# Layer norms' last step on VectorE or ScalarE, and a new order for a two-layer graph network

## The chip, the cores and the metric

The kernel runs on one core of a Trainium2 chip. The metric is the device time of one execution in microseconds (us), and the median of several executions is quoted. The core's engines work side by side, each through its own list of instructions in order: TensorE (PE in the profile, its weight loads PEld), VectorE (DVE), ScalarE (ACT), GpSimd (POOL) and SyncE (SP), which only issues DMAs here.

## The reference

Two graph layers run one after the other over 16 graphs of 1024 nodes with 256 features. The second layer has two attention steps and a feed-forward network.

```python
# layer 0, w = 16, n = 1024, d = 256, H = 8 heads of 32
q, k, v = heads(features @ Wq), heads(features @ Wk), heads(features @ Wv)
e = einsum(q, k); e = where(e >= 0, e, 0.2 * e)
attn = softmax(where(adj > 0, e, NEG)); h = attn @ v
out = layernorm(h, g1, b1)
out = concatenate([out, features]) @ Wffn.T
x = layernorm(out, g2, b2) + features
# layer 1, gat: Wh = h @ W, scores = leaky(Wh @ a[:d] + (Wh @ a[d:]).T), softmax over axis 1
h = gat(gat(x, adj, W1, a1), adj, W2, a2)
h = layernorm(x + h, g_ln1, b_ln1)
ff = relu(h @ w_ff1 + b_ff1) @ w_ff2 + b_ff2
out = layernorm(h + ff, g_ln2, b_ln2)
# layernorm: (x - mean) * rsqrt(var + eps) * g + b, over the 256 features
```

There are four layer norms. The first three are followed in the kernel by a transpose, after which gain and offset are applied by column; the last one goes to the output.

## The kernel before, in words

A graph is called a batch `b`. Its 1024 nodes are 8 tiles of 128 rows, or 4 pairs `u` of tiles.

**The work of a batch.** `x_pair` loads and transposes the features, `mask_part` packs the adjacency matrix into an fp8 mask, and `qk_part` and `v_part` make queries, keys and values. Queries and keys go through DRAM and come back as split halves (`load_stacks`). For each of 8 heads and 8 key tiles, `all_scores` makes a 128x1024 score tile on PE (L615). `weights` scales it on ACT (L631), takes the maximum on DVE (L633), takes the exponential on ACT (L636) and multiplies by the mask on POOL (L640). `all_values` multiplies the weights by the values and by minus one (L655), which is done in 32-column pieces ("narrow" in the planner). `join` adds two weight tiles on DVE (L699). `after_head` brings a head's result into `hn`.

Then comes the rest of the batch (`rest`). `rows_pair` normalizes `hn` (first layer norm), transposes it (L372), multiplies by `Wffn` (L792, L795), normalizes the result `y` (second layer norm), transposes it and forms `x1` and the rows of the first attention (L824). `attention` makes a 128x1024 weight tile per node tile on DVE (L877, L880) and scales the rows on ACT (L885). `second_rows` (L915) and `normed_pair` (L940) are the products of the two attentions. `normed_pair` ends with the third layer norm and a transpose into `rT`. `feed_forward` and `hidden` (L980, L986, L989, L1008) work on `rT`, and end in the fourth layer norm, which has lines of its own (L1019, L1021).

**Layer norms.** `stats` makes mean and variance by row on DVE (L350, L352) and the reciprocal deviation `rs` on ACT by a logarithm and an exponential (L355, L357). `normalized` (L361 to L366) then does one DVE instruction per 128x256 tile: subtract the mean, multiply by `rs`. It is called for two tiles at a time, three times per pair `u`: on `hn` and on `y` in `rows_pair`, and on `y` in `normed_pair`. That is 3 x 4 x 16 = 192 calls and 384 tiles.

**What sets the order.** Each engine's list is written before the program runs, by a planner (`Order`). Every piece of work is a thread, a Python generator, that asks for an engine with a planned duration in ns (`on(DVE=320, shared=True)`), for a buffer of a pool (`take`, `give`), or for another thread's event (`wait`, `fire`). Where a thread offers two engines, the planner takes the one that would end first by its own clocks, and the instruction is emitted for that engine. `shared` says that DVE and POOL exclude each other in the plan for that instruction. Among all pieces that could start within 300 ns of the earliest, the one with the smallest due time (`aim`) goes first. The due times are a batch's start plus a table entry times `SLOT` (253 us in the table before): `AIM` for steady batches, `EARLY` for the rest of batches 0 and 1. In the tables, `rows`, `first0/1`, `graph0/1`, `second`, `normed` and `ff` are the stages of `rest`; `x`, `mask`, `qk`, `v` are the next batch's preparation; `fast0`, `fast1` and `fast15` stretch the due times of the scores in those batches; `lead` is how far ahead of its due time a score may go. `ff` has one entry per pair `u`, the wait after the third layer norm before its feed-forward is due. A changed duration or table entry can thus change the order of all five lists.

**Pools.** PSUM has 2 score buffers, 1 accumulator for the values and 3 general ones (`misc`). SBUF has 6 buffers for weights (`p`), 18 small ones (`pair`), and 1 `job`, held by the feed-forward that runs.

Of the kernel before, what the change touches and what calls it, by code (L numbers as in the profile page):

```python
# [14 lines left out]
AF = mybir.ActivationFunctionType  # L15
OP = mybir.AluOpType
# [170 lines left out]
def on(shared=False, delay=0.0, mode=None, **costs):  # L187
    return "on", (costs, shared, delay, mode)
# [22 lines left out]
def start(thread, aim):  # L211
    return "start", (thread, aim)


def aim(time, lead):
    return "aim", (time, lead)
# [17 lines left out]
def unshifted_path(  # L234
# [8 lines left out]
    nc = tc.nc  # L243
# [16 lines left out]
    YW = D + 2  # L260
    NSUM = NT * H + 2 * NT
    NSCORE = 4 * NT
    SLOT = 253e3
    PACE = SLOT / (H * NT // 2)


    AIM = dict(mask0=0.602, x=1.454, x_step=-0.0104, mask=0.9396, mask_step=-0.0101, qk0=0.4907, qk1=1.7441,
               qk_step=-0.0518, v0=0.7416, v1=0.621, v_step=0.0547, rows=-0.079, rows_step=-0.0113, first0=0.2137,
               first1=-0.446, graph0=-0.0793, graph1=0.316, graph_step=0.0481, second=0.7493, second_step=-0.015,
               normed=1.0223, normed_step=-0.0115, ff_wait=(None, 0, 1, 0), ff=(0.5532, 0.1074, 3.6996, 1.0353),  # L270
               ff_step=0.0063, fast0=0.2312, fast1=0.6979, fast15=1.0127, lead=14.8372)

    EARLY = dict(x=2.6481, x_step=-0.1001, mask=0.5019, mask_step=0.0795, qk0=0.7532, qk1=1.2626, qk_step=-0.1325,
                 v0=0.2134, v1=1.5023, v_step=-0.0416, rows=-2.7213, rows_step=-0.3343, first0=-0.8482,
                 first1=-4.695, graph0=0.0441, graph1=-0.9035, graph_step=-0.1073, second=0.463,
                 second_step=0.0554, normed=0.7744, normed_step=0.0342, ff_wait=(None, 0, 1, 0),
                 ff=(2.0875, 0.7055, 1.5112, 0.6358), ff_step=0.0607)

    const = ctx.enter_context(tc.tile_pool(name="const", bufs=1))
    sb = ctx.enter_context(tc.tile_pool(name="sb", bufs=1))  # L280
# [7 lines left out]
    def share(b, name):  # L288
        return (EARLY if b < 2 else AIM)[name]

# [67 lines left out]
        return mv, rs  # L358

    def normalized(dst, srcs, mv, rs):  # L360
        for i, (row, src) in enumerate(zip(dst, srcs)):  # L361
            if row is src:
                yield on(DVE=320, shared=True)
            else:
                yield on(DVE=323)
            nc.vector.tensor_scalar(row, src, mv[:, i, 0:1], rs[:, i:i + 1], op0=OP.subtract, op1=OP.mult)  # L366

    def transposes(pt, srcs):

# [34 lines left out]
    def mask_part(b, t, halves):  # L404

        n = len(halves)
        ints = []
        if b:
            yield take("adj")
        elif halves[0]:  # L410
            yield wait(("mask", b, t, 0))
        for kh in halves:
            yield take("pair")
            ai = buf([P, HALF], "pair", "adj_i", I32)
            ints.append(ai)
            part = adj[b].rearrange("(u p i) k -> u i p k", p=P, i=2)[t // 2, t % 2, :, kh * HALF:(kh + 1) * HALF]
            if b:
                yield pause(1500)
                yield on(ACT=400, delay=3500)
                nc.scalar.dma_start(ai, part)  # L420
            else:
                yield pause(2000)
                yield load()
                nc.sync.dma_start(ai, part)
        yield take("adjb")
        ab = buf([P, 2 * HALF], "adjb", "adj_b", F8)
        for i, ai in enumerate(ints):
            yield on(DVE=336, shared=True)
            nc.vector.tensor_scalar(ab[:, i * HALF:(i + 1) * HALF], ai, 0.0, -1.0,
                                    op0=OP.is_gt, op1=OP.mult, saturate=False)  # L430
            yield give("pair")
        if b:
            yield give("adj")
        yield take("misc")
        pt = misc(BF)
        pairs = ab.bitcast(BF)
        yield on(PE=30 + 140 * n)
        for i in range(2 * n):
            nc.tensor.transpose(pt[:, i * P:(i + 1) * P], pairs[:, i * P:(i + 1) * P], ident_b)
        yield give("adjb")  # L440
        yield on(ACT=46 + 218 * n)
        k0 = 2 * halves[0]
        nc.scalar.copy(masks[b].bitcast(BF).rearrange("p (k q) -> p k q", k=NP)[:, k0:k0 + 2 * n, t * P:(t + 1) * P],
                       pt[:, :2 * n * P].rearrange("p (k q) -> p k q", k=2 * n))
        yield give("misc")
        for kh in halves:
            yield fire(("mask", b, t, kh))

    def make_mask(b, t0):
# [3 lines left out]
        for n, (t, halves) in enumerate(parts):  # L453
            yield start(mask_part(b, t, halves),
                        t0 + ((share(b - 1, "mask") if b else AIM["mask0"]) + share(b - 1, "mask_step") * n) * SLOT)

# [4 lines left out]
    def x_pair(b, u):  # L461
        yield take("pair")
        xr = buf([P, 2, D], "pair", "xr")
        yield pause(1500)
        yield on(ACT=400, delay=3500)
        nc.scalar.dma_start(xr, x[b, u * 2 * P:(u + 1) * 2 * P, :].rearrange("(p i) d -> p i d", p=P))
        yield take("misc")
        pt = misc()
        yield on(PE=460)
        transposes(pt, [xr[:, i, :] for i in range(2)])  # L470
        yield give("pair")
        engine = yield evacuate(2 * D)
        copy(engine, xTs[b][:, :, u * 2 * P:(u + 1) * 2 * P], pt.rearrange("p (c n) -> p c n", c=DC))
        yield give("misc")
        yield fire(("xT", b, u))

    def qk_part(b, g, o, nh):

        w = (wq, wk)[o]
        cols = slice(nh * HALF, (nh + 1) * HALF)  # L480
        for u in range(nh * 2, nh * 2 + 2):
            yield wait(("xT", b, u))
        if b:
            yield take("stage")
        yield take("pair")
        yield take("pair")
        yield take("misc")
        pa = misc()
        high, low = (buf([P, HALF], "pair", n) for n in ("high", "low"))
        yield on(PE=1728)  # L490
        for dc in range(DC):
            nc.tensor.matmul(pa, w[:, dc, g * P:(g + 1) * P], xTs[b][:, dc, cols],  # L492
                             start=(dc == 0), stop=(dc == DC - 1))
        yield on(ACT=466)
        nc.scalar.copy(high.bitcast(FR), pa)
        yield on(DVE=594)
        nc.vector.tensor_tensor(low, pa, high, op=OP.subtract)
        yield give("misc")
        if (b, g) == (0, 1):

            yield wait(("stack", 0, 0))
        yield load(2)
        for i, part in enumerate((high, low)):
            nc.sync.dma_start(scratch[b, g][o, :, i, cols], part)
        yield give("pair")
        yield give("pair")
        if b:
            yield give("stage")
        yield fire(("qk", b, g, o, nh))

    def project_qk(b, g, t0):
        scratch[b, g] = dram.tile([2, P, 2, N], FT, name="qk_halves")
        for o in range(2):
            for nh in range(NH):
                yield start(qk_part(b, g, o, nh), t0 + (2 * o + nh) * share(b - 1, "qk_step") * SLOT)

    def v_part(b, g, u):
        yield wait(("xT", b, u))
        yield take("misc")
        pa = misc()  # L520
        yield on(PE=895)
        for i in range(2):
            for dc in range(DC):
                nc.tensor.matmul(pa[:, i * P:(i + 1) * P], xTs[b][:, dc, (2 * u + i) * P:(2 * u + i + 1) * P],  # L524
                                 wv[:, dc, g * P:(g + 1) * P], start=(dc == 0), stop=(dc == DC - 1))
        engine = yield evacuate(2 * P)

        dst = vs[b, g][:, 2 * u:2 * u + 2, :].rearrange("p t c -> p (t c)")
        src = pa[:, :2 * P]
        if engine == "DVE":  # L530
            nc.vector.tensor_scalar(dst, src, -1.0, None, op0=OP.mult)
        else:
            nc.scalar.activation(dst, src, AF.Copy, scale=-1.0)
        yield give("misc")
        yield fire(("v", b, g, u))

    def project_v(b, g, t0):
        yield take("v")
        vs[b, g] = buf([P, NT, G * DH], "v", "v")
        for u in range(NP):  # L540
            yield start(v_part(b, g, u), t0 + share(b - 1, "v_step") * u * SLOT)

# [6 lines left out]
    def project(b, t0):  # L549
        yield take("xT")  # L550
        xTs[b] = buf([P, DC, N], "xT", "xT")
        for u in range(NP):
            yield start(x_pair(b, u), t0 + (share(b - 1, "x") + share(b - 1, "x_step") * u if b else 0.0) * SLOT)
        yield start(make_mask(b, t0), t0 + (0.5 if b else 0.0) * SLOT)
        for g in range(H // G):
# [35 lines left out]
    def pace(b):  # L591
        return PACE * {0: AIM["fast0"], 1: AIM["fast1"], B - 1: AIM["fast15"]}.get(b, 1.0)

    def all_scores():
        for b in range(B):
# [4 lines left out]
            for h in range(H):  # L600
                yield wait(("stack", b, h))
                q, kk = stacks[b, h]
                for t in range(NT):
                    due = t0 + (h * NT + t) / 2 * pace(b)
                    if b == 0 or t % 2 == 0:
                        yield aim(due, AIM["lead"] * PACE)
                        for _ in range(2 if b else 1):
# [877 lines left out]
```

## Time and profile before

| what | value |
|---|---|
| median of 3 runs | 4314.74 us (4314.66 to 4316.35) |
| the profiled execution's own time | 4317.81 us |
| its span, first to last instruction | 4315.9 us |
| mean granted TensorE clock | 0.990 |
| instructions | 76274 |
| first score of batch 0, 1, 2 | 39.1, 208.0, 468.8 us |
| first score to first score, batches 5 to 15 | 260.1 to 260.4 us each |
| last score | 4089.2 us |

The span is shorter than the execution by 1.9 us. The profile's first part gives each engine's busy time and its share of the span; the second part cuts the span into 40 equal slices and gives the busy share in tenths. Answers by stage give busy time of each engine in a stretch of the span. The waits are idle time of an engine, put down to the instruction that ended it. The groups give, by line, engine and tile, the count, the summed busy time and the mean duration in ns of one instruction.

### The profile page before, as it was taken

To read this page: it belongs to the slowest core of one execution; us is meant where nothing else is said; L and a number is where in the kernel's file an instruction comes from. 1 tells how busy PE (TensorE), PEld (TensorE's weight loads), DVE (VectorE), ACT (ScalarE), POOL (GpSimd) and SP (SyncE) were. 2 spreads that over 40 slices of the span, in tenths; PEclk is the share of its full clock that TensorE was granted. 3 is DMA by queue.
4 is the path that set the end of the run, shared out by engine and by line. 5 is a ranking of instruction groups with operands and counts; after the bars stand their busy time and mean duration, and the time that the engine had idled before them with its cause. 6 is when DMAs were issued, how large, how long until landed. Compare 5 with 4: busy or idle time off the path is not lost.

```text
span 4315.9 us, 76274 instructions
## 1 busy us (share of the span) xinstructions
PE 4189.7 (97%) x30027; PEld 3030.3 (70%) x30027; DVE 3544.8 (82%) x5491; ACT 2942.7 (68%) x4362; POOL 2571.6 (60%) x1161
## 2 busy tenths in 40 slices
PE   8788999999999999999999999999999999999999
PEld 4466677677777777777777777777777777777687
DVE  6878878888888887879879788887889879788853
ACT  6756677777767677776776767677776776767632
POOL 5846467664757656574664757646575674747700
PEclk9999999999999999999999999999999999999999
DMA  6413223322232322323232222322323222222100
GB/s 188 125 54 99 69 76 87 91 72 86 74 94 67 96 84 68 90 71 89 84 84 81 79 81 79 91 73 81 91 74 89 81 84 84 74 79 57 30 20 21
DMA packets 156282, 344.79 MB, mean 80 GB/s; under 512 B 21750, under 2 KB 24332, under 8 KB 155916
## 3 DMA queue, kind: packets, MB, share of 16 engines
q1 hardware_dynamic: 112140, 260.13, 21.0%
q10 hardware_dynamic: 43776, 79.71, 6.6%
q8 instruction: 239, 3.92, 0.4%
q14 instruction: 127, 1.04, 0.1%
HBM read 239.09 MB, written 100.66 MB: 79 GB/s over the span
## 4 chain that ended last, share of the span: by engine, by line
PE 82%; DVE 11%; ACT 3%; POOL 1%; DMA 1%; issue 1%; SPq 0%; ACTq 0%; POOLq 0%; DVEq 0%
PE ps_a L655 17%; PE ps_s L615 11%; PE ps_m L915 10%; PE ps_m L980 9%; PE ps_m L940 9%; PE ps_m L1008 7%; PE ps_m L492 4%; DVE p L633 3%; PE ps_m L792 3%; PE ps_m L824 3%; PE ps_m L795 3%; PE ps_m L524 2%; PE ps_m L372 2%; DVE p L699 2%; POOL p L640 1%; DVE att L880 1%
## 5 line engine op out<-in xcount | busy, mean ns | idle before, releaser
L640 POOL TENSOR_TENSOR p<-p,mask 128x1024 f32<-128x1024 f32 x1024 | 2471.1, 2431 | 1425.5 <-ACT p L636 1044.1
L633 DVE TENSOR_TENSOR p<-p,ps_s 128x1024 f32<-128x1024 f32 x1024 | 1211.3, 1213 | 251.2 <-ACT p L631 248.1
L636 ACT ACTIVATE p<-p 128x1024 f32<-128x1024 f32 x1024 | 1082.2, 1059 | 302.3 <-DVE p L633 276.7
L631 ACT ACTIVATE p<-ps_s 128x1024 f32<-128x1024 f32 x1006 | 986.3, 1021 | 345.2 <-PE ps_s L615 283.0
L615 PE MATMUL ps_s<-qs,ks 128*128 128x512 f32 x2048 | 658.7, 437 | 30.6 <-DVE p L633 27.0
L655 PE MATMUL ps_a<-p,v 128*32 128x256 f32 x8192 | 561.9, 388 | 24.4 <-POOL p L640 24.3
L615 PEld LDWEIGHTS ps_s<-qs,ks 128*128 128x128 f32 x2048 | 352.6, 190 | 266.1 <-issue 114.8
L940 PE MATMUL ps_m<-y,att 128*128 128x256 f32 x2048 | 481.1, 382 | 12.6 <-ACT y L885 11.1
L915 PE MATMUL ps_m<-y,att 128*128 128x258 f32 x2048 | 477.1, 383 | 14.4 <-ACT y L885 12.9
L980 PE MATMUL ps_m<-rT,wf 128*128 128x256 f32 x2048 | 474.3, 383 | 9.4 <-ACT hid L989 4.3
L1008 PE MATMUL ps_m<-wf,hid 128*128 128x256 f32 x2048 | 475.7, 381 | 0.6 <-DVE hid L986 0.6
L915 PEld LDWEIGHTS ps_m<-y,att 128*128 128x128 f32 x2048 | 385.5, 190 | 89.3 <-ACT y L885 13.8
L980 PEld LDWEIGHTS ps_m<-rT,wf 128*128 128x128 f32 x2048 | 381.0, 190 | 85.9 <-issue 14.3
L699 DVE TENSOR_TENSOR p<-p 128x1024 f32<-128x1024 f32 x256 | 410.5, 1604 | 23.6 <-PE ps_a L655 23.4
L940 PEld LDWEIGHTS ps_m<-y,att 128*128 128x128 f32 x2048 | 378.4, 190 | 71.1 <-ACT y L885 11.3
L1008 PEld LDWEIGHTS ps_m<-wf,hid 128*128 128x128 f32 x2048 | 379.1, 190 | 63.6 <-issue 8.2
L655 PEld LDWEIGHTS ps_a<-p,v 128*32 128x32 f32 x8192 | 209.5, 109 | 289.3 <-issue 130.8
L655 PE MATMUL ps_a<-p,minus_ones 128*32 128x256 f32 x6144 | 405.8, 382 | 1.2 <-DVE p L699 1.2
L877 DVE SCALAR_TENSOR_TENSOR att<-first,second 128x1024 f32<-128x1024 f32 x256 | 359.7, 1405 | 32.4 <-ACT first L864 28.3
L880 DVE SCALAR_TENSOR_TENSOR att<-mask,att 128x1024 f32<-128x1024 fp8e4 x256 | 339.5, 1326 | 5.6
L655 PEld LDWEIGHTS ps_a<-p,minus_ones 128*32 128x32 f32 x6144 | 199.1, 111 | 138.3 <-issue 7.9
L885 ACT ACTIVATE y<-y,check 128x258 f32<-128x258 f32 x256 | 131.1, 512 | 220.4 <-DVE check L883 217.9
(101 smaller groups left out, 4330.0 us busy)
## 6 DMA issues: line engine op xcount, KB each, us to landing
qs<-qk_halves SPq DMA_DIRECT2D x256, 256.0 KB, 4.0
ks<-qk_halves SPq DMA_DIRECT2D x256, 256.0 KB, 5.2
adj_i<-in_adj_dram ACTq DMA_DIRECT2D x240, 256.0 KB, 3.1
qk_halves<-high SPq DMA_DIRECT2D x128, 256.0 KB, 2.8
qk_halves<-low SPq DMA_DIRECT2D x128, 256.0 KB, 3.6
xr<-in_x_dram ACTq DMA_DIRECT2D x64, 256.0 KB, 4.7
x_kept<-x SPq DMA_DIRECT2D x64, 256.0 KB, 2.0
x<-x_kept SPq DMA_DIRECT2D x64, 256.0 KB, 5.1
```

What stands on the lines that cost most here:

```text
L615: nc.tensor.matmul(ps[:, cols], kk[:, t * P:(t + 1) * P], q[:, cols], start=True, stop=True)
L631: nc.scalar.activation(p, ps, AF.Copy, scale=ALPHA)
L633: nc.vector.tensor_tensor(p, p, ps, op=OP.max)
L636: nc.scalar.activation(p, p, AF.Exp)
L640: nc.gpsimd.tensor_tensor(p, p, mask_of(b, t), op=OP.mult)
L655: nc.tensor.matmul(acc[i * DH:(i + 1) * DH, at:at + QN].rearrange("d (t r) -> d t r", r=DH), w, p.rearrange("k (t i r) -> k i t r", i=4, r ...
L699: nc.vector.tensor_tensor(ps[to], ps[to], ps[by], op=OP.add)
L880: nc.vector.scalar_tensor_tensor(e, mask_of(b, j), -1.0, e, op0=OP.mult, op1=OP.mult, accum_out=sums[:, j:j + 1])
L915: nc.tensor.matmul(pa[:, cols:cols + width], big[:, j, i * P:(i + 1) * P], rows[:, j, :width], start=(j == 0), stop=(j == NT - 1))
L940: nc.tensor.matmul(pa[:, i * D:(i + 1) * D], big[:, j, t * P:(t + 1) * P], y2[:, j, :D], start=(j == 0), stop=False)
L980: nc.tensor.matmul(pa[:, i * 2 * P:(i + 1) * 2 * P], wf1[:, dc, hc * P:(hc + 1) * P], rT[:, dc, :], start=(dc == 0), stop=(dc == DC - 1))
L1008: nc.tensor.matmul(pa[:, i * D:(i + 1) * D], hid[hc // 2][:, hc % 2, i * P:(i + 1) * P], wf2[:, hc, :], start=(hc == 0), stop=False)
```

## The change

`normalized` first makes, on DVE, a small tensor `shift` of minus mean times reciprocal deviation, in place of the mean. Each tile is then `x * rs + shift`, by DVE (`tensor_scalar`) or by ACT (`activation` with `Identity`, a scale and a bias per row), as the planner chooses. All tiles are now marked `shared` for DVE. `SLOT` and both tables have new numbers.

```diff
-    SLOT = 253e3
+    SLOT = 250e3
     PACE = SLOT / (H * NT // 2)
...
-    AIM = dict(mask0=0.602, x=1.454, x_step=-0.0104, mask=0.9396, mask_step=-0.0101, qk0=0.4907, qk1=1.7441,
-               qk_step=-0.0518, v0=0.7416, v1=0.621, v_step=0.0547, rows=-0.079, rows_step=-0.0113, first0=0.2137,
-               first1=-0.446, graph0=-0.0793, graph1=0.316, graph_step=0.0481, second=0.7493, second_step=-0.015,
-               normed=1.0223, normed_step=-0.0115, ff_wait=(None, 0, 1, 0), ff=(0.5532, 0.1074, 3.6996, 1.0353),
-               ff_step=0.0063, fast0=0.2312, fast1=0.6979, fast15=1.0127, lead=14.8372)
-
-    EARLY = dict(x=2.6481, x_step=-0.1001, mask=0.5019, mask_step=0.0795, qk0=0.7532, qk1=1.2626, qk_step=-0.1325,
-                 v0=0.2134, v1=1.5023, v_step=-0.0416, rows=-2.7213, rows_step=-0.3343, first0=-0.8482,
-                 first1=-4.695, graph0=0.0441, graph1=-0.9035, graph_step=-0.1073, second=0.463,
-                 second_step=0.0554, normed=0.7744, normed_step=0.0342, ff_wait=(None, 0, 1, 0),
-                 ff=(2.0875, 0.7055, 1.5112, 0.6358), ff_step=0.0607)
+    AIM = dict(mask0=0.4699, x=1.5774, x_step=-0.1258, mask=0.8255, mask_step=-0.0072, qk0=0.615, qk1=2.0728,
+               qk_step=-0.1056, v0=0.8087, v1=1.02, v_step=-0.027, rows=-0.1328, rows_step=-0.0385, first0=0.1214,
+               first1=-0.6386, graph0=-0.1709, graph1=0.3188, graph_step=0.0457, second=0.7084,
+               second_step=-0.0261, normed=1.035, normed_step=-0.0035, ff_wait=(None, 0, 1, 0),
+               ff=(0.9008, 0.2745, 5.9697, 1.6613), ff_step=0.0306, fast0=0.0645, fast1=0.8173, fast15=0.9687,
+               lead=18.1388)
+
+    EARLY = dict(x=2.358, x_step=-0.304, mask=0.5282, mask_step=0.1545, qk0=0.6534, qk1=1.4792, qk_step=-0.1653,
+                 v0=0.1742, v1=1.791, v_step=-0.0413, rows=-3.8422, rows_step=-0.442, first0=-1.368,
+                 first1=-4.8515, graph0=0.0558, graph1=-1.2834, graph_step=-0.2577, second=0.3723,
+                 second_step=0.0783, normed=1.1722, normed_step=0.0885, ff_wait=(None, 0, 1, 0),
+                 ff=(3.6871, 0.867, 0.8328, 0.7446), ff_step=0.1804)
...
     def normalized(dst, srcs, mv, rs):
+        shift = mv[:, :, 0]
+        yield on(DVE=110)
+        nc.vector.scalar_tensor_tensor(shift, shift, -1.0, rs, op0=OP.mult, op1=OP.mult)
         for i, (row, src) in enumerate(zip(dst, srcs)):
-            if row is src:
-                yield on(DVE=320, shared=True)
+            engine = yield on(DVE=320, ACT=463, shared=True)
+            if engine == "DVE":
+                nc.vector.tensor_scalar(row, src, rs[:, i:i + 1], shift[:, i:i + 1], op0=OP.mult, op1=OP.add)
             else:
-                yield on(DVE=323)
-            nc.vector.tensor_scalar(row, src, mv[:, i, 0:1], rs[:, i:i + 1], op0=OP.subtract, op1=OP.mult)
+                nc.scalar.activation(row, src, AF.Identity, scale=rs[:, i:i + 1], bias=shift[:, i:i + 1])
```

## The prediction, made before the change was run

> **What bounds the kernel now.** I first read the page: busy time by engine, then the slices.
>
> ```profile
> PE 4189.7 (97%) x30027; PEld 3030.3 (70%) x30027; DVE 3544.8 (82%) x5491; ACT 2942.7 (68%) x4362; POOL 2571.6 (60%) x1161
> ...
> PE   8788999999999999999999999999999999999999
> ...
> PEclk9999999999999999999999999999999999999999
> ```
>
> PE is busy nearly everywhere. DVE, from which the change takes work, has 18% idle. The second view is busy time by stage (columns: length, busy us and instructions of PE, PEld, DVE, ACT and POOL, granted clock, DMA).
>
> ```profile
> 40.00:208.00 168.00, 133.35 (x1124) 63.84 (x1124) 147.23 (x139) 122.30 (x141) 156.63 (x71) 0.90 0.47 130
> 208.00:270.00 62.00, 57.43 (x410) 43.53 (x408) 44.62 (x99) 39.03 (x74) 18.11 (x10) 0.97 0.25 79
> 270.00:300.00 30.00, 17.07 (x89) 11.95 (x89) 24.60 (x35) 16.49 (x21) 13.50 (x7) 0.77 0.16 51
> ...
> 360.00:400.00 40.00, 28.38 (x185) 20.98 (x188) 34.06 (x56) 21.56 (x30) 19.32 (x9) 0.83 0.33 93
> ...
> 1240.00:1500.00 260.00, 258.24 (x1873) 187.79 (x1873) 221.53 (x344) 183.80 (x272) 161.57 (x73) 1.00 0.29 82
> ...
> 4090.00:4316.00 226.00, 212.89 (x1089) 181.75 (x1088) 110.03 (x270) 73.12 (x181) 7.01 (x4) 0.99 0.06 21
> ```
>
> A steady batch takes 260 us, of which PE idles 1.8. Batch 0 (40 to 208) is another regime: PE idles 34.7 us and POOL is 93% busy. Two short holes follow, at 270 and 360, where PE idles and then runs at a lower granted clock. The third view is PE's waits: first from 240 to 400 us, then from 500 to 4000 us by group (the figure after the bar's second part is idle time).
>
> ```profile
> PE ps_m L915 <- ACT y L885: 12.9, 1, 12.9
> PE ps_m L940 <- ACT y L885: 11.1, 1, 11.1
> ```
>
> ```profile
> L615 PE MATMUL ps_s<-qs,ks 128*128 128x512 f32 x1730 | 547.2, 433 | 7.2 <-DVE p L633 5.9
> L655 PE MATMUL ps_a<-p,v 128*32 128x256 f32 x6928 | 467.6, 385 | 6.7 <-POOL p L640 6.6
> ...
> L980 PE MATMUL ps_m<-rT,wf 128*128 128x256 f32 x1728 | 401.9, 383 | 7.0 <-ACT hid L989 4.3 <-ACT z L330 2.6
> ```
>
> The holes are one wait each, for the attention's first rows. In the 3500 us of steady work all waits of PE add up to 27.2 us. No layer norm stands among the large ones.
>
> **The edit to the layer norms.** Rows by form:
>
> ```profile
> L366 DVE TENSOR_SCALAR y<-y,mv,rs 128x256 f32<-128x256 f32 x256 | 151.2, 627 | 16.4 <-ACT rs L357 16.3
> ...
> L391 ACT ACTIVATE rT<-ps_m,columns 128x256 f32<-128x256 f32 x112 | 57.5, 564 | 8.6 <-PE ps_m L372 5.5 <-DVE rT L389 1.9
> ...
> L366 DVE TENSOR_SCALAR hn<-hn,mv,rs 128x256 f32<-128x256 f32 x128 | 46.9, 428 | 0.4 <-ACT rs L357 0.3
> ```
>
> - Removed from DVE, if every tile moved: 151.2 + 46.9 = 198.1 us, 0.516 us a tile. Of the 384 tiles, 331 take 0.41 us in the mean; the other 53 average 1.50 us and nearly all end 0.15 us after a POOL instruction (L640) ends, so they are held up by POOL.
> - Added on DVE: 192 small instructions on 128x2. DVE's 128x2 addition takes 0.154 us and its 128x2 copy 0.156 us, so 192 x 0.155 = 29.8 us, 1.9 us a batch.
> - Added on ACT, per moved tile: between 0.509 us (L747, the same function, SBUF to SBUF, with a bias per row) and 0.564 us (L391, scale and bias per row, out of PSUM). I take 0.54.
> - How many move is the planner's choice. With none, DVE gains 29.8 us of work. With all, DVE loses 168 and ACT gains 384 x 0.54 = 207. DVE is quicker when free, and ACT when DVE is busy or POOL holds it up. I take half: DVE 3545 - 99 + 30 = 3476 us, ACT 2943 + 104 = 3047 us.
> - The chain of each norm gets longer: statistics, `rs`, then `shift` on DVE, then the tile, perhaps back on ACT. That adds about 0.16 us plus an engine hop. Behind a tile on ACT stand score scaling and exponentials; behind `shift` on DVE stand the L633 maxima. PE has other work ready in all these places of a steady batch, so I count it at nothing there.
>
> PE gains and loses no instruction. So the sum is not made of these 30 to 200 us; only what PE waits, or loses by changing over, can change.
>
> A rule speaks against the move. The Trainium skill, "ScalarE: Activation LUTs", section "Rules for kernel authors", says to do multiplications and additions on VectorE, not on ScalarE. The trace agrees on speed alone (0.41 us unhindered against 0.51 to 0.56) but not with the mean of 0.516 that POOL's hold-ups leave. Its section "What ACT_TABLE_LOAD costs" gives 186 ns + 0.833 ns per element + about 93 ns per operand pointer, an estimate of 585 ns here; by that ACT would gain 112 us instead of 104, and the sum below would be the same.
>
> **The new order, term by term.**
> - *Batch 0, 40 to 208 us.* `fast0` falls from 0.23 to 0.06, so its scores come before other work. POOL needs 64 x 2.43 = 155.5 us, against 168 now: at most 11 us to win. PE's preparation for batch 1 can be crowded out by as much (+5). I take -3.
> - *The two holes.* Idle 12.9 and 30 - 17.07 = 12.93 agree for the first; the second idles 40 - 28.38 = 11.6. The low clocks (0.77 over 30 us, 0.83 over 40) cost 6.9 and 6.8 more. Together 38 us. DVE fills the first one with eight attention tiles in a row, 2.65 us each in the timeline; layer norms are only a few us of the chain ahead (16 tiles x 0.41 = 6.6 us). The new due times of `rows` and `first` bring it forward. Bounds -38 and +6; I take -6, nearest to the layer norms' own rows.
> - *Steady waits.* Bounds -27.2 (all gone) and +31 (the rival below). I take -3, a tenth of them.
> - *Changes between wide and narrow products.* In the timeline of PE:
>
> ```profile
> 2011.83 3.62 PE L940 MATMUL ps_m<-y,att 128*128 128x256 f32 x16
> 2015.38 1.07 PE L655 MATMUL ps_a<-p,v 128*32 128x256 f32 x16
> 2016.26 1.48 PE L655 MATMUL ps_a<-p,minus_ones 128*32 128x256 f32 x24
> 2017.67 0.73 PE L615 MATMUL ps_s<-qs,ks 128*128 128x512 f32 x2
> ```
>
>   Sixteen L940 at (3.62 - 0.38) / 15 = 0.216 us are 3.46 us, yet L655 starts 3.55 after: 0.09 to enter. Two products take 0.88, so five should end at 2017.58; the next starts 0.09 later. A visit costs about 0.2 us, and there are 33 in each steady batch. A different order has a different number. Eight visits more or fewer are 8 x 0.2 x 16 = 26 us, my bounds. The later `ff` due times and the longer `lead` leave more to choose from, so I take 1.5 fewer: -5.
> - *The end, 4090 to 4316.* PE is 94% busy and the last 9 us are the fourth layer norm, which isn't edited: 0.
>
> The sum is -3 - 6 - 3 - 5 = -17 us. Against the profiled execution, 4317.8 - 17 = 4300.8. The median lies 3.1 below that execution, so **4298 us**.
>
> **Rivals.**
> - *A, the forecast*, 4298, 4280 to 4306: chance 0.44.
> - *B, the order gains much more.* Half of the holes (-19), half of batch 0's room (-6), a third of the waits (-9), six visits fewer (6 x 0.2 x 16 = -19): -53, 4262. For it: holes and visits are that large. Against it: the steady batch has only 1.8 us of idleness. Chance 0.14.
> - *C, nothing shows.* The edit is off PE's path and the new order is worth no more than the old; or the planner keeps nearly all tiles on DVE. 4306 to 4323, 4313. Chance 0.18.
> - *D, slower: ACT in the score loop.* With two score buffers, PE's next score waits for L631 (1.02 us) and L633 (1.21 us). A moved tile of 0.54 us that stands ahead of L631 delays both. PE already waits for L633 37 times. If 60 of the 384 tiles hit a score for which PE has no substitute, that is 32 us; less the 17 above, +15: 4330. It decides from about 48 such tiles (26 us) on. For it: ACT is found idle until a score arrives 285 times, so the loop is often tight, and the planner's 463 ns must stand for this instruction's whole effect. Against it: PE has much other work in a steady batch. Chance 0.24.
>
> **Numbers.** This kernel's measurement can tell about 0.2%, 8.6 us, from no change. Faster: A and B, nearly all, 0.58. Same: C, 0.18. Slower: D, 0.24. The range reaches from just below B to just above D: 4258 to 4333; it leaves out the outer bounds of holes, visits and waits taken together, under 2 in 10. A's own range is 4280 to 4306.
>
> **What would show it.** Right, if L366 splits into DVE and ACT rows near 0.41 and 0.54 us; if ACT rises towards 3047 us and DVE falls towards 3476; if the steady batch comes down by 0.3 to 0.6 us from 260.2, through fewer narrow visits; and if the holes at 270 and 360 shrink. Wrong, if PE's waits for L633 grow past 27 us (D), if batches 0 to 3 get longer, or if the steady batch moves by several us, which would mean that the order is worth more than I can read from these waits.

## The result, and the profile after

The changed kernel takes **4395.14 us** (median of 3 runs, 4393.93 to 4397.01) against 4314.74: a ratio of 1.0185, 95% interval 1.0171 to 1.0200. It is slower by 80 us, and the prediction (4298, range 4258 to 4333) missed on both sign and size. The profiled execution has a span of 4393.3 us at a granted clock of 0.989, against 4315.9 at 0.990.

First the page of the changed kernel: busy time, and PE's row of slices. Lines are 4 higher than before from the layer norms on (L640 became L644 and so on).

```profile
PE 4206.3 (96%) x30027; PEld 3030.3 (69%) x30027; DVE 3596.6 (82%) x5529; ACT 3014.6 (69%) x4516; POOL 2506.5 (57%) x1161
...
PE   7788999999999999999999999999999999999899
```

DVE, which was to be relieved, has 52 us more to do than before, not 69 us less. The instruction counts of PE are the same; over the span its idle time grows by 61 us and its busy time by 17. Next, busy time by stage: batch 0, the two stretches after it, one steady batch, and the end.

```profile
40.00:203.40 163.40, 130.89 (x1134) 64.74 (x1134) 144.74 (x141) 121.69 (x140) 151.39 (x70) 0.92 0.46 128
...
473.00:744.00 271.00, 255.16 (x1854) 182.78 (x1846) 231.24 (x345) 185.85 (x276) 160.96 (x74) 0.99 0.27 78
...
2317.90:2582.70 264.80, 259.57 (x1876) 187.88 (x1872) 223.91 (x344) 188.94 (x282) 155.31 (x73) 1.00 0.28 80
4163.00:4393.00 230.00, 215.00 (x1096) 182.88 (x1096) 113.48 (x283) 73.57 (x180) 8.65 (x5) 0.99 0.05 19
```

A steady batch now takes 264.8 us from first score to first score, against 260.2, and PE idles 5.2 us in it instead of 1.8. By those first scores: batch 0 is 2.7 us shorter (166.2), batches 1 to 4 are 30 us longer together (270.5, 270.2, 257.0 and 261.3 against 260.8, 258.7, 251.2 and 258.5), batches 5 to 14 are 43 us longer (2644.5 against 2601.8), and the rest, with a first score 2 us earlier, lies in the last batch.

The waits of PE from 500 to 4000 us show where (time in total, times, longest). They add up to 75.3 us instead of 27.2.

```profile
PE ps_s L619 <- DVE p L637: 13.7, 24, 0.9
PE ps_a L659 <- POOL p L644: 12.2, 11, 1.2
PE ps_m L376 <- DVE x L816: 10.0, 12, 1.3
PE ps_m L828 <- DVE check L833: 6.8, 11, 0.6
```

Two of these lines answer to nothing before: there PE waited 0.2 us for the copy into `check` at L824 and not at all at L372 for `x` of L812. They come back 11 or 12 times, one of each per steady batch, at the same place. The groups, with shapes kept apart, show the new and split instructions.

```profile
L364 DVE SCALAR_TENSOR_TENSOR mv<-mv,rs 128x2 f32<-128x2 f32 x192 | 103.4, 539 | 36.2 <-ACT rs L358 36.1
...
L370 ACT ACTIVATE y<-y,mv,rs 128x256 f32<-128x256 f32 x135 | 75.7, 593 | 38.8 <-DVE mv L364 38.7
...
L368 DVE TENSOR_SCALAR y<-y,rs,mv 128x256 f32<-128x256 f32 x121 | 68.5, 601 | 2.4
...
L368 DVE TENSOR_SCALAR hn<-hn,rs,mv 128x256 f32<-128x256 f32 x123 | 52.5, 468 | 2.2
```

The planner moved 140 of the 384 tiles to ACT (135 of `y`, 5 of `hn`), each at 0.59 us. The striking row is the first: a 128x2 instruction with a mean of 0.539 us. Its median is 0.160 us; 64 of the 192 take more than 0.3 us (54 of them more than 0.5), up to 2.1, and these 64 are together 73 us over the median; I call them held up, or long. One of them, in the timeline of a steady batch:

```profile
2359.71 2.13 POOL L644 TENSOR_TENSOR p<-p,mask 128x1024 f32<-128x1024 f32 x1 [5.82 <-ACT p L640]
...
2360.30 1.55 DVE L364 SCALAR_TENSOR_TENSOR mv<-mv,rs 128x2 f32<-128x2 f32 x1 [0.27 <-ACT rs L358]
2360.32 1.04 PE L828 MATMUL ps_m<-w,x 128*128 128x260 f32 x4
2361.77 0.14 DVE L833 COPY check<-ps_m 128x2 f32<-128x2 f32 x1
2361.89 1.09 ACT L370 ACTIVATE y<-y,mv,rs 128x256 f32<-128x256 f32 x2 [1.35 <-DVE mv L364]
2361.97 1.14 PE L828 MATMUL ps_m<-w,x 128*128 128x260 f32 x4 [0.61 <-DVE check L833]
```

POOL starts a mask multiplication at 2359.71 and ends it at 2361.84. `shift` starts on DVE at 2360.30 and ends at 2361.85. Behind it in DVE's list stands the small copy out of PSUM that frees PE's buffer, so PE waits 0.61 us, and two tiles on ACT wait 1.35 us. The long `shift` instructions end a median of 0.017 us after one of POOL's ends: 78 of the 192 start while POOL runs an instruction, and not one of the 78 ends before that one has. So the theory (H): **`shift` reads two tensors from SBUF, is held up until POOL's running instruction ends, and holds up the lists behind it.** Its rivals: the new order is worse by itself (O), tiles on ACT delay score scaling as the prediction's rival D had it (A), and any unforeseen work costs as much (U).

### The profile page after: what moved, and what is told of

Its sections match the earlier page's. It is cut to its first block, busy times and chain, and to the rows that moved or that the text cites. A ratio compares the mean times of both kernels' runs of the same rounds, so it can differ in the third digit from the quotient of the medians.

```text
span 4393.3 us, 76572 instructions
## 1 busy us (share of the span) xinstructions
PE 4206.3 (96%) x30027; PEld 3030.3 (69%) x30027; DVE 3596.6 (82%) x5529; ACT 3014.6 (69%) x4516; POOL 2506.5 (57%) x1161
## 4 chain that ended last, share of the span: by engine, by line
PE 77%; DVE 13%; ACT 4%; issue 3%; POOL 2%; DMA 1%; ACTq 0%; SPq 0%; POOLq 0%; DVEq 0%
PE ps_a L659 16%; PE ps_s L619 10%; PE ps_m L919 10%; PE ps_m L984 9%; PE ps_m L1012 8%; PE ps_m L944 8%; PE ps_m L496 4%; DVE p L637 3%; PE ps_m L528 2%; PE ps_m L796 2%; POOL p L644 2%; PE ps_m L799 2%; PE ps_m L376 2%; PE ps_m L828 2%; DVE att L884 1%
## 5 line engine op out<-in xcount | busy, mean ns | idle before, releaser
L644 POOL TENSOR_TENSOR p<-p,mask 128x1024 f32<-128x1024 f32 x1024 | 2416.0, 2378 | 1554.3 <-ACT p L640 1125.7
L637 DVE TENSOR_TENSOR p<-p,ps_s 128x1024 f32<-128x1024 f32 x1024 | 1214.3, 1212 | 260.7 <-ACT p L635 257.9
L640 ACT ACTIVATE p<-p 128x1024 f32<-128x1024 f32 x1024 | 1082.1, 1059 | 309.7 <-DVE p L637 285.7
L619 PE MATMUL ps_s<-qs,ks 128*128 128x512 f32 x2048 | 657.6, 437 | 57.1 <-DVE p L637 56.5
L619 PEld LDWEIGHTS ps_s<-qs,ks 128*128 128x128 f32 x2048 | 352.8, 190 | 270.2 <-issue 97.4
```

Of the source, the lines that this page charges most:

```text
L619: nc.tensor.matmul(ps[:, cols], kk[:, t * P:(t + 1) * P], q[:, cols], start=True, stop=True)
L637: nc.vector.tensor_tensor(p, p, ps, op=OP.max)
L640: nc.scalar.activation(p, p, AF.Exp)
L644: nc.gpsimd.tensor_tensor(p, p, mask_of(b, t), op=OP.mult)
```

## The experiments

Each ratio is to executions of the kernel before on the same chip as the run (medians of 4312.4, 4316.8 and 4312.9 us on the three chips). Where one instruction's place in a profile is compared, it is one execution against another; executions of one kernel differ by several us.

**Without the shift instruction, same order.** In the changed kernel only this goes; the planner still sees its 110 ns, so all lists stay as they are.

```diff
         yield on(DVE=110)
-        nc.vector.scalar_tensor_tensor(shift, shift, -1.0, rs, op0=OP.mult, op1=OP.mult)
```

> The changed kernel's five lists exactly, but without the 192 instructions that make shift (the offset used is the plain mean, so the result is not the layer norm). Theory H (shift is held up by POOL: 55 of 192 last about 1.5 us, 103 us in all instead of 30, and everything behind it on DVE moves): 4315 to 4335 us, steady batch near 260.5 us. Theory O (the new order is worse by itself): 4375 to 4395, steady batch 264 to 265. Theory A (tiles on ACT ahead of score scaling, the rival D of the prediction): 4370 to 4390, since the 140 ACT tiles stay.

Measured: 4314.92 us, ratio 1.0003 (0.9993 to 1.0012), steady batch 259.8 us. The whole 80 us go with 192 tiny instructions. The 140 tiles on ACT and the new tables are still there, so O and A fall as causes by themselves. A stretch of 260 us of steady work:

```profile
2000.00:2260.00 260.00, 258.31 (x1874) 188.51 (x1874) 216.08 (x333) 189.04 (x283) 155.70 (x73) 1.00 0.29 82
```

PE idles 1.7 us in it, against 1.9 before the change, although DVE has 5 us less to do than before (220.98 in the same stretch) and ACT 5.5 us more (183.54 there). That is what the offload itself is worth to PE: nothing that shows.

**Another instruction of the same length in its place.** This takes away the hold-up and keeps the place, the count, the chain and the duration.

```diff
-        nc.vector.scalar_tensor_tensor(shift, shift, -1.0, rs, op0=OP.mult, op1=OP.mult)
+        nc.vector.reciprocal(shift, rs)
```

> The changed kernel's order and instruction count, but the 192 shift instructions are reciprocals of the same 128x2 tile rs, a form that POOL never held up (the offset used is the reciprocal of rs, so the result is not the layer norm). Theory H (the cost is the hold-up): durations all near 0.17 us and 4315 to 4330 us. Rival U (any work on DVE that the plan's 110 ns and its clocks do not foresee costs as much): near 4340 to 4395, since the instruction still stands in the chain between rs and the tile.

The values of this run send the program, after its first part, through its general path as well, so the whole execution takes 17647 us. The first part ends with a small matmul for that decision, on a tile of ones; its place in the timeline of PE is the time to compare. Before the change it starts at 4306.75 us, after it at 4383.36, without `shift` at 4306.27. With reciprocals:

```profile
4308.81 0.19 PE L1188 MATMUL ps_m<-ones,got 128*1 128x1 f32 x2
```

```profile
L364 DVE RECIPROCAL mv<-rs 128x2 f32<-128x2 f32 x192 | 30.2, 158 | 36.5 <-ACT rs L358 36.4
```

The median is 0.159 us in place of 0.160, the longest is 0.168 in place of 2.095, and 74.6 of the 76.6 us are gone. Again 78 of the 192 start while POOL runs, and 76 of these end before POOL does. H is shown: the cost is the hold-up, not the instruction.

**Shift by column.** One tensor operand in place of two.

```diff
-        nc.vector.scalar_tensor_tensor(shift, shift, -1.0, rs, op0=OP.mult, op1=OP.mult)
+        for i in range(len(srcs)):
+            nc.vector.tensor_scalar(mv[:, i, 0:1], mv[:, i, 0:1], rs[:, i:i + 1], -1.0, op0=OP.mult, op1=OP.mult)
```

> The changed kernel's order, but shift is made by two DVE instructions with one tensor operand of 128x1 each, in place of one with two tensor operands of 128x2. Theory H, if this form is not held up (as the 128x1 reciprocals and the statistics never were): 384 x 0.16 = 61 us of DVE instead of 103, no long ones, 4320 to 4350. If this form is held up too: 4395 to 4440, with durations up to 2 us. Theories O and A: 4385 to 4400 either way.

Measured: 4342.65 us, ratio 1.0064 (1.0047 to 1.0081), within H's range.

```profile
L365 DVE TENSOR_SCALAR mv<-mv,rs 128x1 f32<-128x1 f32 x384 | 62.7, 205 | 35.5 <-ACT rs L358 35.4
```

None is held up (0.166 to 0.216 us), though 154 of the 384 start while POOL runs. Still, two of 0.205 us per call in place of one of 0.16 cost about 28 us against the run without `shift`. H holds for the hold-up; U has a share, too: the lists have little room for time that the plan did not set aside.

**Shift in the kernel before.** Order unchanged, all tiles on DVE.

```diff
+        shift = mv[:, :, 0]
...
+            if i == 0:
+                nc.vector.scalar_tensor_tensor(shift, shift, -1.0, rs, op0=OP.mult, op1=OP.mult)
-            nc.vector.tensor_scalar(row, src, mv[:, i, 0:1], rs[:, i:i + 1], op0=OP.subtract, op1=OP.mult)
+            nc.vector.tensor_scalar(row, src, rs[:, i:i + 1], shift[:, i:i + 1], op0=OP.mult, op1=OP.add)
```

> The kernel before with its order unchanged, all tiles on DVE, with the one shift instruction put ahead of each pair of tiles, and multiply-add in place of subtract-multiply. Theory H: shift is held up here too, +30 to +80 us: 4345 to 4395. Theories O and A: the order is the old one and no tile is on ACT, so only 30 us of idle DVE are used: 4313 to 4325.

Measured: 4349.74 us, ratio 1.0083 (1.0066 to 1.0100), within H's range and above that of O and A. The decision's matmul stands at 4341.67, 34.9 us later than before.

```profile
L368 DVE SCALAR_TENSOR_TENSOR mv<-mv,rs 128x2 f32<-128x2 f32 x192 | 80.9, 421 | 14.1 <-ACT rs L357 13.9
```

```profile
PE ps_m L795 <- DVE x L815: 7.4, 11, 0.7
```

43 of the 192 are held up, 51 us over the median together. From 500 to 4000 us PE now waits 11 times for `x`, which stands behind them on DVE; before, its products with `Wffn` (L792, here L795) never waited for `x`.

**Reciprocals in the kernel before.** The same, with `nc.vector.reciprocal(shift, rs)`.

> The kernel before with its order, with 192 reciprocals of 128x2 that the plan does not foresee where the run before_with_shift had shift instructions (the offset used is the reciprocal of rs, so the result is not the layer norm). Theory H: none is held up, 192 x 0.17 = 33 us of DVE that mostly lies in idle time, 4313 to 4325. Rival U: as slow as with shift, 4345 to 4355.

The decision's matmul stands at 4326.34 us (4306.75 before): 19.6 us. Neither expectation was met.

```profile
L368 DVE RECIPROCAL mv<-rs 128x2 f32<-128x2 f32 x192 | 30.1, 157 | 13.9 <-ACT rs L357 13.7
```

Steady batches keep their 260.1 us, so 30 us of unforeseen work that is not held up costs nothing in the steady state. The difference is in batches 0 to 4, which take 1217.0 us together against 1198.1. How much of that is the reciprocals is not shown, because single executions scatter there: the changed lists take 1203.8 us for these batches without `shift`, 1207.0 with reciprocals and 1196.7 in the run further down that is as fast as the kernel before.

The steady batch repeats far better, and gives the price of the hold-ups in both sets of lists. In the old lists three `shift` instructions are held up in each, 3.9 us together, and the batch takes 261.1 us, 1.0 more than with reciprocals. In the changed lists four are held up, 4.2 us together, and the batch takes 264.8 us, 4.9 more than with reciprocals (259.9). So nearly the same time of hold-ups costs five times as much in one set of lists as in the other. The waits show what stands behind the hold-ups; no run gives a rule for their price.

**Shift on ACT.** The changed order; nothing of `shift` on DVE.

```diff
-        nc.vector.scalar_tensor_tensor(shift, shift, -1.0, rs, op0=OP.mult, op1=OP.mult)
...
             if engine == "DVE":
-                nc.vector.tensor_scalar(row, src, rs[:, i:i + 1], shift[:, i:i + 1], op0=OP.mult, op1=OP.add)
+                nc.vector.tensor_scalar(row, src, mv[:, i, 0:1], rs[:, i:i + 1], op0=OP.subtract, op1=OP.mult)
             else:
+                shift = mv[:, i, 0:1]
+                nc.scalar.activation(shift, shift, AF.Copy, scale=-1.0)
+                nc.scalar.activation(shift, shift, AF.Copy, scale=rs[:, i:i + 1])
```

> The changed kernel's order and a full layer norm: DVE tiles subtract the mean and multiply by rs as before and need no shift; for each of the 140 ACT tiles two small ACT instructions make it (140 x 2 x 0.2 = 56 us of ACT that the plan does not foresee). Theory H: no instruction of shift on DVE, so 4315 to 4335. Rival U: 56 us unforeseen, on an engine that score scaling waits for, 4340 to 4395.

Measured: 4368.13 us, ratio 1.0118 (1.0101 to 1.0135), steady batch 264.0.

```profile
L370 ACT ACTIVATE mv<-mv,rs 128x1 f32<-128x1 f32 x140 | 41.3, 295 | 4.5
L369 ACT ACTIVATE mv<-mv 128x1 f32<-128x1 f32 x140 | 26.8, 191 | 0.0
```

This was a miss for H and a hit for U: 68 us on ACT that the plan did not know cost about 50, with no `shift` on DVE to be held up. The 140 tiles of 0.59 us that the plan did know cost nothing that shows (the run without `shift` has them).

**Half of the change: new layer norms, old tables.** The diff is the change without its tables.

> The changed layer norms with the old SLOT, AIM and EARLY, so the planner makes a third order. Theory O (the new tables are worse than the old): 4315 to 4335. Theory H: as slow as the changed kernel, 4380 to 4400, since shift is still there. A third possibility, that due times fit only the durations they were made for: 4400 or more, with a steady batch above 264.8 us.

Measured: 4457.12 us, ratio 1.0334 (1.0317 to 1.0352). The time is that of the third possibility. Batches 8 to 13 take between 256.6 and 287.6 us; they never become regular. 59 of the 192 `shift` instructions are held up here too, so this run does not tell the tables from the hold-ups.

**The other half: old layer norms, new tables.** The changed kernel with `normalized` as it was before.

> The old layer norms (all on DVE, no shift) with the new SLOT, AIM and EARLY: the other half of the change alone, a fourth order. If the new tables make a good order by themselves: below 4330. If due times fit only the durations they were made for, as the run with the old tables and the new norms (4457 us) suggests: 4390 to 4470, with a steady batch above 264 us and no shift to blame.

Measured: 4408.04 us, ratio 1.0211 (1.0194 to 1.0228), steady batch 265.9, with no `shift` at all, as the second expectation had it. The new due times make a good order with the new durations (4314.92 in the first run) and a bad one with the old. So the tables can't be judged by planning again with the other layer norms, and the runs that keep the five lists are the ones that can tell.

**What is left of the change without hold-ups.** The changed lists, a full layer norm, and `shift` by the one-operand form only for the tiles that go to ACT. The 140 places come from a constant string.

```diff
-        nc.vector.scalar_tensor_tensor(shift, shift, -1.0, rs, op0=OP.mult, op1=OP.mult)
+        for i in range(2):
+            if plan[i] == "A":
+                nc.vector.tensor_scalar(mv[:, i, 0:1], mv[:, i, 0:1], rs[:, i:i + 1], -1.0, op0=OP.mult, op1=OP.mult)
         for i, (row, src) in enumerate(zip(dst, srcs)):
...
-                nc.vector.tensor_scalar(row, src, rs[:, i:i + 1], shift[:, i:i + 1], op0=OP.mult, op1=OP.add)
+                nc.vector.tensor_scalar(row, src, mv[:, i, 0:1], rs[:, i:i + 1], op0=OP.subtract, op1=OP.mult)
```

> The changed kernel's order and a full layer norm: shift is made on DVE in the form that was never held up (one tensor operand, 128x1, 0.205 us), and only for the 140 tiles that go to ACT; DVE tiles subtract and multiply as before. 140 x 0.205 = 28.7 us, about what the plan set aside. Theory H: what is left of the change without hold-ups, 4310 to 4325 us, so the offload is worth nothing to PE. If moving tiles to ACT has a value that hold-ups hid: below 4305. Rival U (any instruction that stands elsewhere than planned costs as much as it lasts): 4330 to 4345.

Measured: 4316.10 us, ratio 1.0004 (0.9995 to 1.0013), within H's range.

```profile
L373 DVE TENSOR_SCALAR mv<-mv,rs 128x1 f32<-128x1 f32 x140 | 23.3, 202 | 16.5 <-ACT rs L358 16.4
```

It is as fast as the kernel before and 79 us faster than the changed one. None of the 140 is held up, though 135 start while POOL runs. The idea does what it says once `shift` is not held up, and gains nothing.

**Planning around POOL.** The shift instruction is marked `shared` in the plan, and the tables are searched anew.

```diff
-        yield on(DVE=110)
+        yield on(DVE=110, shared=True)
```

> The changed layer norms with the shift instruction marked as one that excludes POOL in the plan, and SLOT, AIM and EARLY searched anew for that by small random steps (some 8800 of them). Theory H: the plan then keeps shift clear of POOL, few are held up and the order runs as planned, 4330 to 4360, between the kernel before and the changed one. If hold-ups can't be planned away: 4390 or more, with as many long shift instructions as now.

Measured: 4374.96 us, ratio 1.0143 (1.0127 to 1.0158).

```profile
L353 DVE SCALAR_TENSOR_TENSOR mv<-mv,rs 128x2 f32<-128x2 f32 x192 | 86.6, 451 | 9.2 <-ACT rs L347 7.8
```

The time lies between the two expectations and in neither. 57 are still long: the mark did not keep them clear of POOL in the execution. How much of the 62 us is the hold-up and how much a short search is not told apart.

## Why the prediction was wrong, step by step

- **The step that failed is "Added on DVE: 192 small instructions on 128x2 ... 192 x 0.155 = 29.8 us".** It measured 103.4 us, 73 of them hold-ups by POOL. I priced the instruction by rows of its size (an addition on 128x2 that runs once, a copy from PSUM) and not by rows of its kind. The profile before had the kind: `scalar_tensor_tensor` on SBUF tensors alone, in the fourth layer norm.

```profile
L1021 DVE SCALAR_TENSOR_TENSOR z<-z,rs,bl 128x256 f32<-128x256 f32 x128 | 90.8, 709 | 3.2 <-ACT rs L357 1.5
...
L1019 DVE SCALAR_TENSOR_TENSOR z<-z,mv,gl 128x256 f32<-128x256 f32 x128 | 86.3, 674 | 0.0
```

  Their medians are 480 and 479 ns; the means of 709 and 674 are hold-ups: 28 and 41 of the 128 take more than 0.6 us, and these end a median of 0.28 us after one of POOL's ends. The same prediction said of 53 tiles that POOL holds them up and did not carry it over to the instruction that it added. The diff had a sign of it, too: the tiles are `shared`, the new instruction is not.
- **The step after it failed with it**: "so I count it at nothing there". The cover was thought of as work for PE. What stood behind `shift` was a copy that frees a PSUM buffer (L833), `x` (L816) and the tile on ACT: PE waits 75.3 us from 500 to 4000 us in place of 27.2. With reciprocals in place of `shift` they add up to 31.9.
- **Half of the tiles move**: 140 of 384, 0.59 us each in place of 0.54. ACT rose to 3015 us (predicted 3047); DVE rose to 3597 (predicted 3476). The prediction's 0.516 us a tile counts the overlap of two neighbours once; its own two groups (331 of 0.41, 53 of 1.50) average 0.56.
- **The terms of the order, -17 us**, came to nothing: the run of what is left of the change without hold-ups (4316.10 us) gives them together, as 0.04% +- 0.09%. Batch 0 (predicted -3) takes 168.9 us before and 167.0 in that run, but the runs with the changed lists, which differ from each other in nothing so early, give 166.2 to 170.4, so this shows nothing. The two holes (predicted -6) stayed: waits of 12.9 and 11.1 us before, and in that run, from 240 to 400 us:

```profile
PE ps_s L629 <- DVE p L647: 14.0, 2, 11.7
PE ps_m L954 <- ACT y L899: 11.3, 1, 11.3
```

  A steady batch took 259.9 us in place of 260.2 (predicted -3 for waits and -5 for visits over the run), but not by the way I named: there were 34 visits a batch, one more than before. The median shows none of it.
- **Rival D** had the right sign and the wrong mechanism. Its sign did appear: PE's waits for the maximum (L633, now L637) grew from 27.0 to 56.5 us. But they are 50.4 us in that same run of 4316.10 us, which takes as long as the kernel before, and 11.7 of them are the first hole, now put down to the maximum. Tiles on ACT that the plan knows cost nothing that shows. The price is real where the plan does not know of the work: 68 us on ACT cost about 50 us.
- **The other signs of being wrong** appeared as well: batches 1 to 3 got longer, and a steady batch moved by 4.6 us. The prediction read such a move as the worth of the order; the runs that keep the lists show that it was the hold-ups.
- **The range** allowed +31 us for the waits as a whole. It left out that one instruction's price could be three times its nearest row.

## What to carry to other kernels

Price an added instruction by rows of its kind (its operands and where they lie), and look at the spread between the median and the mean of that row, before its size. In this kernel the lists are fixed in advance and the bounding engine idles 2 us in 260. There, moving work off another engine gained nothing, while a microsecond that the plan did not know cost anything from nothing to a microsecond of the whole. Due times that were found for one set of durations did not fit another, so undo a part by keeping the lists and not by planning again.

## What the runs showed of the hardware

In these runs a DVE instruction that reads two tensors from SBUF waits for POOL's running tensor operation even when it is tiny: 128x2, median 0.160 us, up to 2.095 us. In the same places, the reciprocal of one 128x2 tensor (0.119 to 0.168 us) and a `tensor_scalar` on one 128x1 tensor with a scalar per row (0.166 to 0.216 us) were never held up, although `tensor_scalar` on 128x256 is (0.41 us, up to 2.3). The instructions with one operand in PSUM never were either: L637 takes 1.17 to 1.22 us in all 1024 cases, L816 0.45 to 0.49 in all 128.

The Trainium skill, "SBUF — State Buffer", section "Who interferes with whom", says that a DVE instruction with two SBUF inputs contends with a GpSimd instruction that reads SBUF, and that one with at most one such input, outside the two-port modes, does not. The runs agree, with 73 us of hold-ups of `shift` for the first kind and none for the reciprocals and the 128x1 form. In which mode `tensor_scalar` on 128x256 ran, no run here shows.
